# One core, a conv + FFT + FFN hybrid: the nonlinearity's parts in tiles of one writer each, the pooled sum moved to ScalarE, and a new order of issue

## The chip, the cores and the metric

The kernel runs on one core of a Trainium2 chip. The metric is the device time of one execution in microseconds (us), lower is better. Engines are named as in the profile: PE (TensorE matmul), PEld (TensorE weight load), DVE (VectorE), ACT (ScalarE), POOL (GpSimd), SP (SyncE, which here only issues DMAs).

## What is computed

32 images of 56 x 56 pixels with 96 channels go through two layers, all in float32 except for a quantised feed-forward part. The reference, cut to what matters:

```python
# layer 0, per image: mixture weights from the pooled image
pooled = mean(x, axis=(1, 2))
rw = sigmoid(pooled @ Wr + br)                      # 4 experts
h = relu(bn(x @ Wk(rw) + rw @ bpw))                 # 96 -> 384
h = relu(bn(depthwise3x3(h, sum_e rw_e * Wdw_e)))   # 384 channels
x = bn(h @ Wk2(rw) + rw @ bpwl) + x                 # 384 -> 96
# layer 1, tokens t = x as (3136, 96)
u = relu(bn(layernorm(t) @ w1))                     # 96 -> 192
X = fft(u, over the 3136 tokens)
xr = relu(X.real * rd - X.imag * idg + rb)          # rd, idg: diagonals
xi = relu(X.imag * rd + X.real * idg + ib)
t = t + bn(ifft(xr + 1j * xi).real @ w2)            # 192 -> 96
n = layernorm(t)
t = t + qlinear(relu(qlinear(n, W1)), W2)           # 96 -> 384 -> 96, fp8 e5m2 operands
```

## The kernel before

The image is the outer loop of every stage, and several images are in flight at once, each in another stage. The stages of one image, with the names that the profile shows:

- `mixing`: the image `x` is summed over its 3136 pixels (`pooled`), spread over 128 partitions (`pool_b`), multiplied by `wr_s` on PE (`ps_rw`, one small matmul per image, so it marks the beat of the loop), passed through Sigmoid, and turned into the mixed weights `wk`, `small` and `wk2` by DVE.
- `expansion`: `ps_pw` on PE, evacuated by ACT with Relu into `hp` (128 channels x 34 columns x 56 rows, three channel chunks, half an image `p` at a time).
- depthwise: five of the seven blocks of channel chunks 0 and 1 run as 32 x 32 matmuls with diagonal weights on PE (`ps_dw`, three waves of 144 matmuls per image, evacuated by four ACT Relus each into `h2`; the trace calls it `h`). Chunk 2 and two blocks of chunk 1 run on DVE: ACT makes the first tap, DVE adds eight more with `scalar_tensor_tensor` (`h<-hp,small,h`, sizes 1792, 1344 and 896), ACT applies the Relu.
- `projection`: `ps_pwl`, added to the image by DVE.
- `forward` (two streams, each with every other strip of an image): transposes `ps_t_a`, statistics `st_a`, `dm_a`, `rstd_a`, matmul `ps_w` (`w1c`), `ha` on DVE, first DFT `ps_a`, `g` by ACT, out to DRAM (`gd`).
- `frequencies`: `g2` comes back from DRAM (`g<-gd`), the second DFT `ps_b` runs in two groups of frequencies (16 and 13) and three `kind`s of 128 rows each, and the nonlinearity above follows: ACT makes two affine images of the real part and `|idg * im|`, DVE two multiply-adds with the imaginary part, POOL one addition, ACT a Relu, DVE two final operations into `z`. `spectrum` then multiplies by `w2` (`ps_w<-w_s,z`) and makes the first inverse DFT (`ps_c`, via `zo`, to DRAM as `yd`).
- `inverse` (two streams): `yt` from DRAM, `ps_d`, the second layernorm (`ps_t_f`, `st_f`, `nt`, `ps_n`, `n`), the feed-forward (`ps_f` with three hidden chunks `h` that go ACT copy, DVE bias and Relu, POOL cast to fp8, then PE again), the sum, and the store.

PSUM is one pool of four buffers of two banks, shared by all stages: every matmul group takes one, and it comes free when ACT or DVE has evacuated it.

What sets the order: engines execute their queues in order, and the queues are filled by a planner (`class Plan`) at build time. Each stage is a generator that yields the engine it wants next, the events it needs and the buffers it takes. `Plan.run` always takes the stream that could start first by the planner's own costs (`Engine.__getattr__`), with `SLACK` per engine deciding what counts as a tie, and the stream's `priority` number breaking ties. `arrives` gives the planned landing of a DMA. `psum` (line 322 and on) fills each gap that the planner expects on PE: for a planned gap above 0.3 us it issues one filler matmul (112 x 112, result unused) per 0.19 us into the PSUM buffer that was just taken, ahead of the real matmul. The planner's costs are fixed per operation; for a DVE `scalar_tensor_tensor` of n elements they are 0.13 + n / 960 us.

In the nonlinearity before, both parts of a kind share two tiles: `z` (real and imaginary results side by side) and `mir` (two buffers, real and imaginary side by side). ACT writes the real half of `mir`, DVE the imaginary half, and one ACT Relu (n = 896) covers both. The wait is stated in the code:

```python
yield ACT, [("im", n, kind)]
A.activation(m[:, 0:nk, :], m[:, 0:nk, :], AF.Relu)
```

and PE may not start `ps_b` of group n before the last matmul that reads `z` of group n - 1:

```python
yield PE, [("g2 here", n)] + [("z read", n - 1)] * (n >= 1), 1
```

Nearly all instructions are recorded through one helper, so DVE, ACT and POOL work has line L289 and matmuls L585 (transposes L589, fillers L328). Groups are told apart by tile names.

Of the kernel before, what the change touches and what calls it, by code (L numbers as in the profile page):

```python
# [40 lines left out]
F32 = mybir.dt.float32  # L41
# [7 lines left out]
C = 96  # L49
# [84 lines left out]
class Plan:  # L134
# [7 lines left out]

    TAIL = {PE: 0.2, DVE: 0.12, ACT: 0.14, POOL: 0.1, SP: 0.0}


    SLACK = {PE: 0.05, DVE: 0.2, ACT: 0.1, POOL: 1.2, SP: 0.0}

    def __init__(self, **buffers):
        self.free = dict.fromkeys((PE, DVE, ACT, POOL, SP), 0.0)
# [26 lines left out]
        self.buffers[tag].append(self.now if at is None else at)  # L176
        self.buffers[tag].sort()

    def release_after(self, n, used):

        used.append(self.now)
        if len(used) == n:
            self.release(at=max(used))

    def idle(self):

# [62 lines left out]
class Engine:  # L249
# [12 lines left out]
    def __getattr__(self, name):  # L262
        def issue(out, *args, **kw):
            n, port = _size(out), self.port
            if self.engine == DVE:
                us = 0.13 if n > 32 else 0.08
                if name in ("tensor_reduce", "bn_stats"):
                    n = _size(args[0])
                    us = 0.06 if name == "bn_stats" else us
                elif name == "tensor_scalar" and out.dtype == F16:  # L270
                    n, port = n / 4, True
                us += n / 960.0
            elif self.engine == ACT:
                us = 0.05 if name == "copy" else 0.24 if {"scale", "bias"} <= kw.keys() else 0.15
                us += n / 1200.0
                if {"scale", "bias"} <= kw.keys():
                    us = max(us, 0.36)

                asked = [f for f in args[1:] if f in (AF.Sqrt, AF.Sigmoid)]
                if asked and asked != self.loaded:  # L280
                    us += 1.28
                    self.loaded = asked
            elif self.engine == POOL:
                port = name != "memset"
                us = 0.1 + n * {"tensor_copy": 1.04, "memset": 0.6}.get(name, 2.3) / 1000.0
            else:
                us = 0.36
            self.plan.tick(self.engine, us, port)
            return getattr(self.namespace, name)(out, *args, **kw)  # L289

        return issue
@with_exitstack
def kernel(
# [274 lines left out]
    def as_halves(ap):  # L568
        return ap.rearrange("p (j t) -> p j t", j=2)

    plan = Plan(ps=4, mir=2, zo=1, h16=4, x1=NX1)

    V, W, A, P, Q = (
        Engine(plan, DVE, nc.vector), Engine(plan, DVE, nc.vector, True), Engine(plan, ACT, nc.scalar),
# [14 lines left out]
        nc.tensor.transpose(to, ap, eye)  # L589

    def arrives(nbytes, *key):
        plan.done(*key, late=1.4 + nbytes / 220e3)

    mixed, small_of, wk2s, gds, yds, zs, x1s = {}, {}, {}, {}, {}, {}, {}

# [9 lines left out]
    def mixing():  # L605

        for b in range(NB):
            yield DVE, [("x", b)] + [("x1", b - 2, s) for s in range(NS) if b >= 2]
            pooled = mixp.tile([C, 1], F32, tag="pooled", name=f"pooled_{b}")
            V.tensor_reduce(pooled, xs[b], AX.X, ALU.add)  # L610
            pool_b = mixp.tile([C, 128], F32, tag="pool_b", name=f"pool_b_{b}")
            V.behind.tensor_scalar(pool_b, ones, pooled, 1.0 / N, ALU.mult, ALU.mult)
# [23 lines left out]
            small_of[b] = small  # L636
            plan.done("wk", b)
            for c in range(NPE):
                plan.spawn("diagonals", 3, diagonals(b, c))
            yield DVE  # L640
            wk2 = mixp.tile([128, NC3, C], F32, tag="wk2", name=f"wk2_{b}")
            V.tensor_scalar_mul(wk2, wpwl_s[:, 0], rw[:, 0:1])
# [32 lines left out]
    def expansion():  # L675

        for b, p, before in parts_of_all():
            xb = xpad[b % 2]
            for c in (2, 0, 1):

                for part, (at, ns) in enumerate((((0, (9, 9)), (18, (8, 8))), ((0, (8, 8)), (16, (9,))))[p]):
                    yield PE, [("wk", b)] + (readers(*before, c) if before else []), 1
                    wk = mixed[b]
                    ps = psum(f"ps_pw_{b}_{p}_{c}_{part}")
                    for j, n in enumerate(ns):
                        lo = (G * BW * p + at + j * n) * S
                        mm(
                            ps[:, 512 * j : 512 * j + n * S],
                            wk[:, 128 * c : 128 * c + 128],
                            xb[:, lo : lo + n * S],  # L690
                        )
                    plan.spawn("evac pw", 3, expanded(b, p, c, part, at, ns, ps))
            plan.done("exp", b, p)

    def expanded(b, p, c, part, at, ns, ps):
# [14 lines left out]
    def convolved_tensor():  # L710

        for b, p, before in parts_of_all():
            for i, wave in enumerate(WAVES[p]):
# [21 lines left out]

                plan.tick(PE, 0.4)
                plan.done("dwt", b, p, i)
                plan.spawn("evac dw", 6, convolved(b, p, i, wave, ps))

    def convolved(b, p, i, wave, ps):  # L740
        for q, (c, k) in enumerate(wave):
# [38 lines left out]
    def projection():  # L780

        for b, p, _ in parts_of_all():
            needs = [("h2t", b, p, i) for i in range(len(WAVES[p]))] + [("wk2", b)]
            needs += [("h2v", b, p, c) for c, *_ in ON_VECTOR[p]]
            for s, blocks in (((0, (0, 1)), (1, (2, 3))), ((2, (4, 5)), (3, (6,))))[p]:
# [3 lines left out]
                for c in range(NC3):  # L789
                    for j, k in enumerate(blocks):  # L790
# [150 lines left out]
    def frequencies():  # L941


        n = 0
        flat = g2.rearrange("p k m -> p (k m)")
        for b in range(NB):
            for i, (k0, nk) in enumerate(GROUPS):
                for kind in range(NKIND):
                    yield PE, [("g2 here", n)] + [("z read", n - 1)] * (n >= 1), 1
                    ps = psum(f"ps_b_{b}_{k0}_{kind}")  # L950
                    size = (nk + (kind < 2)) // 2
                    for j in range(size):
                        at = 2 * CH * j + 128 * kind
                        mm(ps[:, 128 * j : 128 * j + PB], flat[:, at : at + 128], dftb_s)
                    plan.spawn("nonlinearity", 4, nonlinearity(n, b, k0, size, kind, ps))
                plan.done("g2", n)
                plan.spawn("spectrum", 4, spectrum(n, b, i, k0, nk))
                n += 1

    def nonlinearity(n, b, k0, nk, kind, ps):  # L960
        rd, idg, rb, ib = (nl_s[:, j, kind : kind + 1] for j in range(4))
        nr = nrd[:, kind : kind + 1]
        re = slots(ps, 128, nk, 128, S)
        im = ps[:, 0 : nk * 128].rearrange("p (n w) -> p n w", w=128)[:, :, S:PB]
        yield ACT
        zt = sp.tile([128, GK, PB], F32, tag=f"z_{kind}", name=f"z_{b}_{k0}_{kind}")
        zs[n, kind] = zt
        zr, zi = zt[:, 0:nk, 0:S], zt[:, 0:nk, S:PB]
        A.activation(zi, re, AF.Identity, scale=idg, bias=ib)
        first = k0 == 0 and kind < 2  # L970
        if first:
            A.activation(zr, re, AF.Identity, scale=rd, bias=rb)
# [5 lines left out]
        used = []  # L978
        m = sp.tile([128, GK, PB], F32, tag="mir", name=f"mir_{b}_{k0}_{kind}", bufs=2)
        mr, mi = m[:, 0:nk, 0:S], m[:, 0:nk, S:PB]  # L980
        plan.spawn("imaginary parts", 0, imaginary_parts(n, kind, im, zi, mi, rd, nr, used))
        if not first:
            A.activation(zr, re, AF.Identity, scale=rd, bias=rb)
# [11 lines left out]
        plan.release("mir")  # L995
        plan.done("z", n, kind)

    def imaginary_parts(n, kind, im, zi, mi, rd, nr, used):
        yield DVE
        V.scalar_tensor_tensor(mi, im, nr, zi, ALU.mult, ALU.add)  # L1000
        V.behind.scalar_tensor_tensor(zi, im, rd, zi, ALU.mult, ALU.add)
        plan.release_after(2, used)
        plan.done("im", n, kind)

    def spectrum(n, b, i, k0, nk):

        for at in range(0, nk, GK):
            some = min(GK, nk - at)
            needs = [("z", n, kind) for kind in range(NKIND)] + [("y", n - 1)] * (n >= 1)
# [40 lines left out]
    def inverse(parity):  # L1050


        for b in range(NB):
            for s in range(parity, NS, 2):
# [47 lines left out]
                for c in range(NC3):  # L1102
                    yield PE, (), 1
                    ps = psum(f"ps_f1_{b}_{s}_{c}")
                    for j in range(2):
# [5 lines left out]
                    plan.spawn("hidden", 2, hidden(parity, b, s, c, ps, h8))  # L1111
# [163 lines left out]
```

## Time and profile before

| | us |
|---|---|
| median of three runs | 4427.69 (4416.8 to 4431.31) |
| the profiled execution, own time | 4422.13 |
| its span in the profile | 4420.3 |
| PE busy | 4143.1 |
| DVE busy | 3481.1 |
| ACT busy | 2596.1 |
| POOL busy | 1097.7 |
| PE busy / span, 0 to 215 us | 166.17 / 215.00 |
| PE busy / span, 215 to 4149 us | 3724.15 / 3934.00 |
| PE busy / span, 4149 to 4420 us | 252.83 / 271.00 |

The middle row pair is the loop at full depth; the first and the last rows are the pipeline filling and draining. One image takes about 133 us there (the small matmul `ps_rw` comes at 2194.6, 2326.3 and 2460.9 us). "Busy" merges overlapping instructions of one engine. A matmul in float32 shows as two records in the profile.

### The profile page before, as it was taken

The numbers are of one execution on the slowest core, as the hardware profiler recorded it, in microseconds if no ns is written. First come the engines' busy times: TensorE is split into PE (matmuls) and PEld (weight loads), VectorE is DVE, ScalarE is ACT, GpSimd is POOL, SyncE is SP. The second block draws the span as 40 slices with busy tenths as digits, with TensorE's granted clock in tenths as the row PEclk, the third lists the DMA queues.
The fourth block names the chain that finished last, engine by engine and source line by source line (L and its number), as shares of the span: only waits on it lengthen the run. The fifth ranks groups of instructions, "written<-read, shape, count | busy, mean of one in ns | idle before, by whom it ended". The sixth has DMA issues, their size and how long they took to land.

```text
span 4420.3 us, 119618 instructions
## 1 busy us (share of the span) xinstructions
PE 4143.1 (94%) x50924; PEld 2786.6 (63%) x50924; DVE 3481.1 (79%) x7224; ACT 2596.1 (59%) x4103; POOL 1097.7 (25%) x1015
## 2 busy tenths in 40 slices
PE   6989999999999999999999999999999999999999
PEld 4556666666666666666666666666666666665678
DVE  6778787878787888787787788787888788888763
ACT  2455666656565656566556666556666556666554
POOL 2012232222232221332222332222332222332222
PEclk9999999999999999999999999999999999999999
DMA  3343344433434433444433443433444433434431
GB/s 87 75 105 83 90 100 105 99 104 82 102 97 105 99 103 79 106 99 99 103 92 84 109 103 98 107 88 88 105 107 102 103 92 85 115 96 102 98 98 51
DMA packets 336040, 424.85 MB, mean 96 GB/s; under 512 B 134928, under 2 KB 254544, under 8 KB 332208
## 3 DMA queue, kind: packets, MB, share of 16 engines
q1 hardware_dynamic: 333172, 417.00, 37.6%
q8 instruction: 401, 6.57, 0.6%
q14 instruction: 131, 1.07, 0.1%
q10 hardware_dynamic: 2336, 0.20, 0.0%
HBM read 202.60 MB, written 205.06 MB: 92 GB/s over the span
## 4 chain that ended last, share of the span: by engine, by line
PE 55%; DVE 18%; ACT 12%; DMA 8%; issue 4%; POOL 2%; SPq 0%; ACTq 0%; POOLq 0%; DVEq 0%
PE ps_w L585 11%; PE ps_dw L585 8%; PE ps_pwl L585 8%; DVE h L289 8%; PE ps_pw L585 8%; PE ps_b L585 6%; DMA g<-gd 5%; PE ps_d L585 4%; ACT nt L289 3%; ACT h L289 3%; DVE z L289 3%; DVE ha L289 3%; DMA gd<-g 2%; PE ps_f L585 2%; POOL h L289 2%
## 5 line engine op out<-in xcount | busy, mean ns | idle before, releaser
L289 DVE SCALAR_TENSOR_TENSOR h<-hp,small,h 128x1792 f32<-128x1792 f32 (+2 forms) x768 | 1318.1, 1716 | 56.9 <-ACT h L289 43.6
L585 PE MATMUL ps_dw<-hp,diag 32*32 32x448 f32 x27648 | 884.1, 545 | 31.5 <-issue 26.2
L289 POOL CAST h<-h 128x784 fp8e5<-128x784 f16 x384 | 544.5, 1443 | 1389.1 <-DVE h L289 1387.5
L585 PEld LDWEIGHTS ps_dw<-hp,diag 32*32 32x32 f32 x27648 | 524.8, 103 | 330.9 <-issue 136.8
L585 PE MATMUL ps_pw<-x,wk 96*128 96x448 f32 (+1 forms) x1344 | 594.5, 567 | 12.5 <-ACT y L289 12.0
L289 ACT ACTIVATE hp<-ps_pw,small 128x896 f32<-128x896 f32 (+2 forms) x384 | 360.4, 947 | 385.9 <-PE ps_pw L585 385.5
L585 PE MATMUL ps_pwl<-h,wk 128*96 128x448 f32 x1344 | 528.0, 540 | 0.3 <-ACT hp L289 0.2
L585 PE MATMUL ps_b<-dftb_s,g 112*128 112x112 f32 x2816 | 372.0, 295 | 45.0 <-DMA g<-gd 37.5
L585 PEld LDWEIGHTS ps_w<-w_s,z 128*112 128x112 f32 (+1 forms) x2816 | 352.6, 178 | 88.1 <-ACT h L289 55.2
L585 PEld LDWEIGHTS ps_b<-dftb_s,g 112*128 112x128 f32 x2816 | 356.8, 209 | 81.5 <-ACT h L289 40.5
L585 PE MATMUL ps_w<-w_s,z 128*112 128x96 f32 (+2 forms) x2816 | 372.3, 286 | 33.0 <-ACT h L289 32.4
L585 PEld LDWEIGHTS ps_pwl<-h,wk 128*96 128x96 f32 x1344 | 213.8, 163 | 263.0 <-issue 262.2
L289 ACT ACTIVATE nt<-yt,nm,rstd_f 112x96 fp8e5<-112x96 f32 x896 | 331.3, 456 | 69.6 <-DVE nm L289 69.2
L585 PEld LDWEIGHTS ps_pw<-x,wk 96*128 96x128 f32 x1344 | 238.8, 191 | 200.8 <-issue 140.5
L585 PE MATMUL ps_w<-w1c,x 96*64 96x192 f32 x3584 | 340.3, 332 | 2.4 <-ACT g L289 1.4
L289 ACT ACTIVATE z<-ps_b,nl_s 128x448 f32<-128x448 f32 (+2 forms) x384 | 248.6, 692 | 159.8 <-PE ps_b L585 159.7
L289 ACT CAST h<-ps_f 128x784 f16<-128x784 f32 x384 | 292.7, 820 | 84.3 <-PE ps_f L585 81.8
L289 DVE SCALAR_TENSOR_TENSOR ha<-ps_w,rstd_a,nshift 128x192 f32<-128x192 f32 x896 | 309.7, 407 | 25.8 <-PE ps_w L585 21.5
L289 POOL TENSOR_TENSOR mir<-mir,z 128x448 f32<-128x448 f32 (+1 forms) x192 | 203.7, 1061 | 482.0 <-ACT mir L289 364.3
L289 POOL TENSOR_TENSOR x<-x,y 96x784 f32<-96x784 f32 x128 | 258.1, 2021 | 261.5 <-DVE y L289 261.5
L289 ACT ACTIVATE h<-ps_dw,small 128x448 f32<-128x448 f32 x384 | 223.5, 628 | 134.6 <-PE ps_dw L585 134.6
L289 DVE SCALAR_TENSOR_TENSOR x<-ps_pwl,small,x 96x896 f32<-96x896 f32 (+1 forms) x128 | 131.5, 1027 | 209.2 <-PE ps_pwl L585 209.2
(167 smaller groups left out, 5727.3 us busy)
## 6 DMA issues: line engine op xcount, KB each, us to landing
gd<-g SPq DMA_DIRECT2D x448, 192.0 KB
g<-gd SPq DMA_DIRECT2D x64, 672.0 KB
x<-in_x_dram SPq DMA_DIRECT2D x32, 1176.0 KB
x<-x SPq DMA_DIRECT2D x128, 294.0 KB
yt<-yd SPq DMA_DIRECT2D x128, 294.0 KB
out_dram<-x SPq DMA_DIRECT2D x128, 294.0 KB
g<-gd SPq DMA_DIRECT2D x64, 546.0 KB
x<-x SPq DMA_DIRECT2D x96, 336.0 KB
```

What stands on the lines that cost most here:

```text
L289: return getattr(self.namespace, name)(out, *args, **kw)
L585: nc.tensor.matmul(to, lhsT, rhs, start=start, stop=stop)
```

## The change

Four things change, and the order of issue follows from all of them, since the planner decides it:

1. The nonlinearity writes four tiles per kind, `nl0` to `nl3`, contiguous, two buffers each, with one writer engine at a time per part. The real and the imaginary part are two independent chains, each with its own Relu on ACT (12 Relus of half the size per image in place of 6) and its own final operation into `z`. The correction `dc` of the zero frequency becomes two additions of one column instead of one addition of two. `z` is taken only when its final operation is issued, and only that operation waits for the reader of the group before; PE's `ps_b` keeps this wait for the last of the three kinds alone.
2. `pooled` comes from an ACT copy of `x` onto itself with an accumulator output, in place of a DVE reduction.
3. The planner multiplies every cost but PE's matmuls (which tick directly) by `MARGIN = 1.07`; SLACK of DVE goes from 0.2 to 0.3 and of ACT from 0.1 to 0.05; a DMA is planned at 2.0 us + bytes / 190e3 per us instead of 1.4 us + bytes / 220e3.
4. Most priorities get other numbers.

The diff, cut to its core:

```diff
+    MARGIN = 1.07
+
-    SLACK = {PE: 0.05, DVE: 0.2, ACT: 0.1, POOL: 1.2, SP: 0.0}
+    SLACK = {PE: 0.05, DVE: 0.3, ACT: 0.05, POOL: 1.2, SP: 0.0}
...
-            self.plan.tick(self.engine, us, port)
+            self.plan.tick(self.engine, us * self.plan.MARGIN, port)
...
-    plan = Plan(ps=4, mir=2, zo=1, h16=4, x1=NX1)
+    plan = Plan(ps=4, nl=2, zo=1, h16=4, x1=NX1)
...
-        plan.done(*key, late=1.4 + nbytes / 220e3)
+        plan.done(*key, late=2.0 + nbytes / 190e3)
...
-            yield DVE, [("x", b)] + [("x1", b - 2, s) for s in range(NS) if b >= 2]
+            yield ACT, [("x", b)] + [("x1", b - 2, s) for s in range(NS) if b >= 2]
...
-            V.tensor_reduce(pooled, xs[b], AX.X, ALU.add)
+            A.activation(xs[b], xs[b], AF.Copy, accum_out=pooled)
+            yield DVE
...
-                plan.spawn("diagonals", 3, diagonals(b, c))
+                plan.spawn("diagonals", 7, diagonals(b, c))
...
-                    plan.spawn("evac pw", 3, expanded(b, p, c, part, at, ns, ps))
+                    plan.spawn("evac pw", 6, expanded(b, p, c, part, at, ns, ps))
...
-                plan.spawn("evac dw", 6, convolved(b, p, i, wave, ps))
+                plan.spawn("evac dw", 1, convolved(b, p, i, wave, ps))
...
-                plan.spawn("evac prj", 6, projected(b, s, blocks, ps))
+                plan.spawn("evac prj", 2, projected(b, s, blocks, ps))
...
-                    yield PE, [("g2 here", n)] + [("z read", n - 1)] * (n >= 1), 1
+                    yield PE, [("g2 here", n)] + [("z read", n - 1)] * (n >= 1 and kind == 2), 1
...
+        u, w, mr, mi = (
+            sp.tile([128, GK, S], F32, tag=f"nl{j}", name=f"nl{j}_{b}_{k0}_{kind}", bufs=2)[:, 0:nk]
+            for j in range(4)
+        )
+        used, over = [], []
+        A.activation(w, re, AF.Identity, scale=idg, bias=ib)
+        imaginary = imaginary_parts(n, b, k0, nk, kind, im, w, mi, used, over)
+        if k0 == 0 and kind < 2:
+            A.activation(u, re, AF.Identity, scale=rd, bias=rb)
             yield DVE
             n0 = CH - 128 if kind else 128
-            at0 = zt[:n0, 0, 0 : S + 1 : S]
-            V.tensor_add(at0, at0, dc[:n0, kind, :])
-        yield ACT, (), "mir"
+            V.tensor_add(u[:n0, 0, 0:1], u[:n0, 0, 0:1], dc[:n0, kind, 0:1])
+            V.tensor_add(w[:n0, 0, 0:1], w[:n0, 0, 0:1], dc[:n0, kind, 1:2])
...
         A.activation(mr, im, AF.Abs, scale=idg)
         plan.release_after(2, used)
         yield POOL
-        P.tensor_add(mr, mr, zr)
-        yield ACT, [("im", n, kind)]
-        A.activation(m[:, 0:nk, :], m[:, 0:nk, :], AF.Relu)
-        yield DVE
-        W.scalar_tensor_tensor(zr, zr, 2.0, mr, ALU.mult, ALU.max)
-        W.scalar_tensor_tensor(zi, zi, 0.0, mi, ALU.max, ALU.subtract)
+        P.tensor_add(mr, mr, u)
+        yield ACT
+        A.activation(mr, mr, AF.Relu)
+        yield DVE, [("z read", n - 1)] * (n >= 1)
+        zr = spectrum_of(n, b, k0, kind)[:, 0:nk, 0:S]
+        W.scalar_tensor_tensor(zr, u, 2.0, mr, ALU.mult, ALU.max)
+        plan.release_after(2, over, "nl")
+        plan.done("z", n, kind, 0)
+
+    def imaginary_parts(n, b, k0, nk, kind, im, w, mi, used, over):
         yield DVE
+        V.scalar_tensor_tensor(mi, im, nrd[:, kind : kind + 1], w, ALU.mult, ALU.add)
+        V.behind.scalar_tensor_tensor(w, im, nl_s[:, 0, kind : kind + 1], w, ALU.mult, ALU.add)
         plan.release_after(2, used)
+        yield ACT
+        A.activation(mi, mi, AF.Relu)
+        yield DVE, [("z read", n - 1)] * (n >= 1)
+        zi = spectrum_of(n, b, k0, kind)[:, 0:nk, S:PB]
+        W.scalar_tensor_tensor(zi, w, 0.0, mi, ALU.max, ALU.subtract)
...
-            ("loads", 8, loads()), ("mixing", 6, mixing()), ("inverse", 1, inverse(0)),
-            ("inverse", 0, inverse(1)), ("frequency loads", 0, frequency_loads()),
-            ("frequencies", 1, frequencies()), ("forward", 0, forward(0)),
-            ("forward", 0, forward(1)), ("projection", 7, projection()),
-            ("vector", 5, convolved_vector()), ("tensor", 2, convolved_tensor()),
-            ("expansion", 7, expansion()),
+            ("loads", 2, loads()), ("mixing", 5, mixing()), ("inverse", 6, inverse(0)),
+            ("inverse", 0, inverse(1)), ("frequency loads", 4, frequency_loads()),
+            ("frequencies", 6, frequencies()), ("forward", 0, forward(0)),
+            ("forward", 1, forward(1)), ("projection", 8, projection()),
+            ("vector", 6, convolved_vector()), ("tensor", 2, convolved_tensor()),
+            ("expansion", 9, expansion()),
```

`spectrum_of` makes the `z` tile of a kind at its first use, and `release_after` gets the buffer's tag as an argument. In the built programs the matmuls of the stages are the same in number; the order is not (nearly every row differs), and the fillers go from 467 to 794.

More of the change, by code (lines that the diff above doesn't have):

```diff
@@ L177, in release, with release_after @@
         self.buffers[tag].sort()
-    def release_after(self, n, used):
+    def release_after(self, n, used, tag="ps"):
         used.append(self.now)
         if len(used) == n:
-            self.release(at=max(used))
+            self.release(tag, max(used))
     def idle(self):
@@ L607, in mixing @@
         for b in range(NB):
-            yield DVE, [("x", b)] + [("x1", b - 2, s) for s in range(NS) if b >= 2]
+            yield ACT, [("x", b)] + [("x1", b - 2, s) for s in range(NS) if b >= 2]
             pooled = mixp.tile([C, 1], F32, tag="pooled", name=f"pooled_{b}")
-            V.tensor_reduce(pooled, xs[b], AX.X, ALU.add)
-            pool_b = mixp.tile([C, 128], F32, tag="pool_b", name=f"pool_b_{b}")
-            V.behind.tensor_scalar(pool_b, ones, pooled, 1.0 / N, ALU.mult, ALU.mult)
+            A.activation(xs[b], xs[b], AF.Copy, accum_out=pooled)
+            yield DVE
+            pool_b = mixp.tile([C, 128], F32, tag="pool_b", name=f"pool_b_{b}", bufs=1)
+            V.tensor_scalar(pool_b, ones, pooled, 1.0 / N, ALU.mult, ALU.mult)
             rw = mixp.tile([128, NE + 1], F32, tag="rw", name=f"rw_{b}")
@@ L954, in frequencies @@
                         mm(ps[:, 128 * j : 128 * j + PB], flat[:, at : at + 128], dftb_s)
-                    plan.spawn("nonlinearity", 4, nonlinearity(n, b, k0, size, kind, ps))
+                    plan.spawn("nonlinearity", 3, nonlinearity(n, b, k0, size, kind, ps))
                 plan.done("g2", n)
-                plan.spawn("spectrum", 4, spectrum(n, b, i, k0, nk))
+                plan.spawn("spectrum", 3, spectrum(n, b, i, k0, nk))
                 n += 1
@@ L961, in nonlinearity @@
         rd, idg, rb, ib = (nl_s[:, j, kind : kind + 1] for j in range(4))
-        nr = nrd[:, kind : kind + 1]
         re = slots(ps, 128, nk, 128, S)
         im = ps[:, 0 : nk * 128].rearrange("p (n w) -> p n w", w=128)[:, :, S:PB]
[L965 to L972, printed above, removed]
+        yield ACT, (), "nl"
+        u, w, mr, mi = (
[7 more added lines that the diff above has]
+            A.activation(u, re, AF.Identity, scale=rd, bias=rb)
             yield DVE
             n0 = CH - 128 if kind else 128
-            at0 = zt[:n0, 0, 0 : S + 1 : S]
-            V.tensor_add(at0, at0, dc[:n0, kind, :])
-        yield ACT, (), "mir"
[L978 to L983, printed above, removed]
+            V.tensor_add(u[:n0, 0, 0:1], u[:n0, 0, 0:1], dc[:n0, kind, 0:1])
+            V.tensor_add(w[:n0, 0, 0:1], w[:n0, 0, 0:1], dc[:n0, kind, 1:2])
+            yield ACT
+            plan.spawn("imaginary parts", 5, imaginary)
+        else:
+            plan.spawn("imaginary parts", 2, imaginary)
+            A.activation(u, re, AF.Identity, scale=rd, bias=rb)
         A.activation(mr, im, AF.Abs, scale=idg)
@@ L988, in nonlinearity, with spectrum_of @@
         yield POOL
-        P.tensor_add(mr, mr, zr)
-        yield ACT, [("im", n, kind)]
-        A.activation(m[:, 0:nk, :], m[:, 0:nk, :], AF.Relu)
-        yield DVE
-        W.scalar_tensor_tensor(zr, zr, 2.0, mr, ALU.mult, ALU.max)
-        W.scalar_tensor_tensor(zi, zi, 0.0, mi, ALU.max, ALU.subtract)
-        plan.release("mir")
-        plan.done("z", n, kind)
-    def imaginary_parts(n, kind, im, zi, mi, rd, nr, used):
-        yield DVE
-        V.scalar_tensor_tensor(mi, im, nr, zi, ALU.mult, ALU.add)
-        V.behind.scalar_tensor_tensor(zi, im, rd, zi, ALU.mult, ALU.add)
-        plan.release_after(2, used)
-        plan.done("im", n, kind)
+        P.tensor_add(mr, mr, u)
[7 more added lines that the diff above has]
+    def imaginary_parts(n, b, k0, nk, kind, im, w, mi, used, over):
+        yield DVE
+        V.scalar_tensor_tensor(mi, im, nrd[:, kind : kind + 1], w, ALU.mult, ALU.add)
+        V.behind.scalar_tensor_tensor(w, im, nl_s[:, 0, kind : kind + 1], w, ALU.mult, ALU.add)
+        plan.release_after(2, used)
+        yield ACT
+        A.activation(mi, mi, AF.Relu)
+        yield DVE, [("z read", n - 1)] * (n >= 1)
+        zi = spectrum_of(n, b, k0, kind)[:, 0:nk, S:PB]
+        W.scalar_tensor_tensor(zi, w, 0.0, mi, ALU.max, ALU.subtract)
+        plan.release_after(2, over, "nl")
+        plan.done("z", n, kind, 1)
+    def spectrum_of(n, b, k0, kind):
+        if (n, kind) not in zs:
+            zs[n, kind] = sp.tile([128, GK, PB], F32, tag=f"z_{kind}", name=f"z_{b}_{k0}_{kind}")
+        return zs[n, kind]
     def spectrum(n, b, i, k0, nk):
@@ L1008, in spectrum @@
             some = min(GK, nk - at)
-            needs = [("z", n, kind) for kind in range(NKIND)] + [("y", n - 1)] * (n >= 1)
+            needs = [("z", n, kind, j) for kind in range(NKIND) for j in range(2)] + [("y", n - 1)] * (n >= 1)
             yield PE, needs + [("yt read", b - 2, s) for s in range(NS) if b >= 2], 1
@@ L1110, in inverse @@
                         )
-                    plan.spawn("hidden", 2, hidden(parity, b, s, c, ps, h8))
+                    plan.spawn("hidden", 1, hidden(parity, b, s, c, ps, h8))
                 yield PE, [("h8", b, s, c) for c in range(NC3)], 1
```

## The prediction

> **What bounds the kernel now.** I read the page's first part, then two stretches of one image each, then PE's waits over the loop at full depth, then the groups by shape that the change touches.
>
> ```profile
> PE 4143.1 (94%) x50924; PEld 2786.6 (63%) x50924; DVE 3481.1 (79%) x7224; ACT 2596.1 (59%) x4103; POOL 1097.7 (25%) x1015
> ...
> PEclk9999999999999999999999999999999999999999
> ```
>
> ```profile
> 2193.40:2267.50 74.10, 70.77 (x724) 48.43 (x723) 64.88 (x136) 48.98 (x77) 20.79 (x21) 1.00 0.31 75
> 2267.50:2326.40 58.90, 55.77 (x855) 35.41 (x853) 44.03 (x90) 33.20 (x55) 13.57 (x11) 1.00 0.49 120
> ```
>
> The columns of the second fence are the stretch and its length, then busy us of PE, PEld, DVE, ACT, POOL, then the clock and DMA. The two rows are one image: the first ends when DVE's last tap of the vector convolution is done, the second at the next `ps_rw`. PE works 126.5 of 133.0 us and sets the beat; DVE is near it in the first part (64.88 of 74.10) and has room in the second (44.03 of 58.90). The clock is full, so filler matmuls have nothing more to win. So the change can only win what PE idles, about 7 us per image. The waits say for whom (us in total, times, longest), from 215 to 4149 us:
>
> ```profile
> PE ps_b L585 <- DMA g<-gd: 33.3, 21, 3.1
> PE ps_w L585 <- ACT h L289: 32.4, 28, 1.5
> PE ps_f L585 <- POOL h L289: 32.0, 28, 1.2
> PE ps_dw L585 <- issue: 24.7, 26, 2.2
> PE ps_t_f L589 <- ACT hp L289: 23.0, 28, 0.9
> PE ps_f L585 <- ACT h L289: 14.7, 60, 1.4
> PE ps_f L585 <- DVE ha L289: 12.4, 28, 0.4
> PE ps_pw L585 <- ACT y L289: 10.9, 16, 1.1
> ...
> PE ps_b L585 <- ACT h L289: 7.1, 5, 2.6
> PE ps_f L585 <- ACT zo L289: 5.6, 28, 0.2
> ```
>
> They add up, with 7.7 us for one late `yt`, to 204 of the 210 us that PE idles in this stretch (3934.00 less 3724.15). No wait is large: each is a transfer or an evacuation that came about 1 us later than the planner thought, once per image (28 times in 29.5 beats). Why the planner is early:
>
> ```profile
> L289 DVE SCALAR_TENSOR_TENSOR h<-hp,small,h 128x1792 f32<-128x1792 f32 x256 | 579.0, 2262 | 7.9 <-ACT h L289 4.3
> ...
> L289 DVE TENSOR_REDUCE pooled<-x 96x1 f32<-96x3136 f32 x32 | 108.9, 3405 | 8.0 <-DMA x<-in_x_dram 8.0
> ...
> L289 ACT ACTIVATE mir<-mir 128x896 f32<-128x896 f32 x96 | 91.1, 949 | 18.8 <-POOL mir L289 17.8 <-DVE mir L289 0.4
> ...
> L289 ACT ACTIVATE h<-h,small 128x1792 f32<-128x1792 f32 x32 | 57.2, 1789 | 230.2 <-DVE h L289 230.2
> ...
> L328 PE MATMUL ps_f<-dftb_s 112*112 112x112 f32 x244 | 26.3, 263 | 0.2 <-ACT h L289 0.2
> ```
>
> The planner gives the 1792-element tap 0.13 + 1792/960 = 2.00 us, the chip took 2.262 (13% more).
>
> **What the Trainium skill says.** "SBUF — State Buffer", section "SBUF: two separate sides": a DVE operation with two SBUF inputs and a GpSimd operation that reads SBUF exclude each other on one shared port for a whole instruction. The trace agrees: taps of 1344 elements took 1.61 us alone and up to 2.1 each (two in 4.29 us) while POOL worked; the planner models the exclusion but starts from too short a cost. "TensorE: Matmul & The Clock Gate", section "What's actually happening", says that PE's clock falls after an idle window of about 3.4 us; the loop's longest wait but one is 3.1 us and the clock is 0.97 to 1.00, so fillers buy nothing. "Perfetto Trace Analysis", section "Optimization Strategy", says that an equal gap that repeats can mean too few buffers; here it is four PSUM buffers whose evacuations queue on ACT.
>
> **The change, part by part.**
>
> Pooled sum. DVE loses 32 x 3.405 = 109 us. ACT gains an operation that the trace doesn't have: "ScalarE: Activation LUTs", section "What ACT_TABLE_LOAD costs", prices immediate operands at 186 ns + 0.833 ns per element, an estimate of 2.80 us for 3136; its price with a pointer operand (280 + 0.833 x 1792 = 1773 ns) meets the trace's 1789. Bounds 2.8 to 3.1 us (plus one small ACT operation like `rstd_f`, 0.29, if the accumulator is read apart); I take 2.8, so 90 us on ACT. In the built order it stands behind the first evacuation of the half image, beside the 4.7 us of `ps_pwl`, with `y` and three `hp` evacuations queued behind it; `ps_rw` and the next `ps_pw` wait for those. Cover gone, it costs PE up to 3 us per image.
>
> Split Relus. 192 of 752 to 949 ns become 384 of half the size: 0.56 us by that page's price, 0.63 by the trace's 448-element rows. Per pair 0.17 to 0.31 us more, I take 0.2: 38 us on ACT. The `dc` additions go from 64 to 128 of 0.155 us: +10 us on DVE. So DVE is 3481 - 109 + 10 = 3382 (76%), ACT 2596 + 90 + 38 = 2724 (62%). PE stays the bound, and neither sum moves the span by itself.
>
> One writer per tile. DVE waited 112.4 us for ACT's `mir` (152 times, waits of all engines): its multiply-add needs only the first ACT operation but stood behind ACT's third. In the new order it waits only for the first. That is 3.5 us of DVE bubbles per image, nearly all in the first part, where DVE is close to PE. It moves the end only through what follows on DVE.
>
> Fillers. In the built order the old loop has none at full depth; the new one has 10 per image, the same for 29 images: 3 ahead of `ps_pw_0_2_0`, 1 ahead of the last spectrum matmul, 6 ahead of `ps_pw_0_1_0`. A filler takes 26.3 / 122 = 0.216 us (244 records are 122 matmuls). 290 x 0.216 = 63 us if PE had other work, nothing if it would have waited; I take 63. The other 37 new ones lie in the fill and the drain, where PE waits for longer: 0.
>
> New order, waits that go. `g<-gd`: a landing takes 9 to 11 us by the chain of waits; the first `ps_b` of an image stood behind one wave (8.7 us) and some 4 us more after the last strip, and now about 30 us later: -33.3. `ps_w<-ACT h`: after a wave the ACT queue held one Relu, then a Relu that waits for DVE's taps, a first tap, and only then the second Relu that frees the PSUM buffer; now the two Relus are adjacent and the waiting one is moved: -32.4. `ps_f<-POOL h`: 7.1 us of PE work between the third hidden matmul and its reader, now 6.7, 12.0, 9.1 and 4.9 in the four places; copy 0.82, bias 0.41 to 0.62, cast 1.44 fit: -32.0. `ps_t_f<-ACT hp`, `ps_pw<-ACT y`, `ps_b<-ACT h`, `ps_f<-ACT zo`: all are buffers freed by an ACT queue that the margin plans later: -23.0 - 10.9 - 7.1 - 5.6. Sum -144.3. Issue (24.7), the three hidden matmuls in a row (14.7 + 12.4) and `yt` stay.
>
> New waits. I walked the new DVE order with the trace's durations from the addition of `ps_d_3` to the last 896-element tap: taps 8 x 1.74 + 8 x 1.15, four `ha` groups 5.5, statistics 5.5, nonlinearity 13.5, biases 5.2, `zo` 2.6, the rest 3.4: 58.8 us. PE has 58.0 us there, and 2.1 of fillers. They are level, so DVE comes in late at a few places: `ps_t_f_2` (0.7), `ps_a_0_0` (0.4), `ps_a_2_4` in the second part (0.6). 1.7 x 29.5 = +50 us.
>
> Sum, against the profiled execution: 4422 - 144 + 63 + 50 = 4391. The median lies 5.6 us above that execution (0.1%), so I say 4395.
>
> **Rivals.**
>
> Slower: DVE becomes the bound of the first part. In the old order it idled 9.2 of these 74.1 us behind in-order waits; if 4 us of such bubbles stay in the new 58.8, DVE needs 62.8 where PE has 60.1, and PE stands at `ps_pw_0_1_0`, behind its six fillers, for the 2.7 us on top: 29.5 x 3 = +89, so 4480. It decides from 1.3 us of bubbles on. For it: the taps still cost 5% more than the planner's cost times 1.07. Against: the freed `mir` wait.
>
> Faster: the fillers fall into waits that would be there anyway and half of the new waits don't come: 4391 - 25 - 31 = 4335, say 4340. For it: two of the three places are where PE waits for the vector taps.
>
> No change: with four PSUM buffers and the same work the 1 us waits form again elsewhere: 4422 - 144 + 144, within 0.3%.
>
> That the new order doesn't do what it says has little room: it is what the build gives.
>
> **How the numbers follow.** Forecast 0.35 (own range 4365 to 4412), faster rival 0.20, no change 0.12, slower rival 0.33. A measurement tells about 0.3% here, 13 us around 4428. So faster 0.55, same 0.12, slower 0.33. The range takes in most of both rivals and ends at 4325 and 4490.
>
> **What would show it.** Right: `ps_b<-DMA`, `ps_w<-ACT h` and `ps_f<-POOL h` gone from PE's waits; TENSOR_REDUCE gone, an ACT row of 2.8 us; DVE's waits for ACT in the nonlinearity well below 112; PE busy near 4206. Wrong: PE waiting for DVE's `h` ahead of `ps_pw`, or for ACT behind the pooled copy, by over 2 us per image.

## The result and the profile after

| | before | after |
|---|---|---|
| median of 20 runs each, us | 4426.01 (4409.01 to 4438.1) | 4443.2 (4424.09 to 4454.81) |
| the profiled execution, own time | 4422.13 | 4424.09 |
| its span | 4420.3 | 4422.3 |

The ratio is 1.0039, 95% interval 1.0029 to 1.005: the change made the kernel 0.4% slower. The forecast was 4395 and faster. The profiled execution of after is the fastest of its 20, 19 us under their median, so its trace shows a mild case of what follows.

The page of after, busy times of the engines and the share of the instruction queue:

```profile
PE 4160.7 (94%) x51578; PEld 2841.8 (64%) x51578; DVE 3385.6 (77%) x7256; ACT 2697.5 (61%) x4360; POOL 968.2 (22%) x1015
...
q8 instruction: 406, 6.65, 0.7%
```

DVE landed within 4 us of the sum made for it (3382), ACT 27 us under its own (2724). PE was busy 17.6 us longer, far less than the forecast's 63. The second line is a DMA queue that brings instructions: packets, MB and the time that they took. PE's records (51578 matmuls and as many weight loads) come to 254 for each of its 406 packets of 16.4 KB, so I take it to be PE's own. It becomes important below.

The loop at full depth, one row of the view by stretches (length, then busy us of PE, PEld, DVE, ACT, POOL, the clock and DMA):

```profile
215.00:4149.00 3934.00, 3733.58 (x46450) 2521.61 (x46452) 3076.41 (x6553) 2465.75 (x3980) 870.63 (x906) 0.99 0.38 97
```

PE idles 200 us in this stretch where it idled 210. PE's longest waits in the same stretch (us in total, times, longest):

```profile
PE ps_dw L587 <- issue: 69.4, 38, 3.9
PE ps_a L587 <- DVE ha L291: 24.2, 29, 0.8
PE ps_d L587 <- DMA yt<-yd: 23.0, 23, 1.9
PE ps_pw L587 <- ACT yt L291: 19.2, 29, 0.7
PE ps_t_f L591 <- DVE x L291: 18.1, 29, 0.7
PE ps_a L587 <- ACT h L291: 12.4, 29, 0.4
PE ps_n L587 <- DVE nl L291: 12.2, 29, 0.4
PE ps_pw L330 <- ACT h L291: 6.8, 29, 0.2
PE ps_w L587 <- ACT h L291: 6.8, 29, 0.2
PE ps_d L587 <- ACT h L291: 3.0, 4, 1.0
PE ps_b L587 <- DMA g<-gd: 0.7, 1, 0.7
```

Read against the list of before, the change did what it set out to do: the waits of `ps_b` for `g`, of `ps_f` for POOL's `h`, and those behind `hp`, `y` and `zo` are gone or nearly so. Two things took their place. One is a set of small waits, most of them exactly once per image (29 times, at most 0.2 to 0.8 us each). The other heads the list: PE stands in the middle of a depthwise wave with no engine and no transfer that it waits for ("issue"), 69.4 us in 38 gaps of up to 3.9 us; before it was 24.7 in 26.

**One such gap.** The timeline of after around one wave (start, length, engine, line, operation, count, in brackets the idle time before it):

```profile
2338.93 0.88 SPq L291 DMA_DIRECT2D g<-gd  x2
2339.28 6.96 PE L587 MATMUL ps_dw<-hp,diag 32*32 32x448 f32 x233
...
2349.08 2.82 PE L587 MATMUL ps_dw<-hp,diag 32*32 32x448 f32 x55 [2.85 <-issue]
```

The view by stretches over the same time:

```profile
2339.00:2343.00 4.00, 4.00 (x138) 2.59 (x138) 2.54 (x8) 1.86 (x3) 0.86 (x2) 1.00 0.68 136
2343.00:2346.20 3.20, 3.20 (x117) 1.92 (x99) 3.16 (x4) 1.09 (x2) 1.13 (x1) 1.00 0.97 172
2346.20:2349.10 2.90, 0.05 (x7) 0.02 (x4) 2.87 (x5) 0.00 (x0) 1.76 (x1) 1.00 0.09 15
```

In the new order SP issues the load of the second frequency group (`g<-gd`, two DMAs of 546 KB, together 1.12 MB) 0.35 us before the wave of the second half image starts. The 16 DMA engines then fill to 97% (the number before the last), and by the time they fall idle PE has stopped, after 233 of the wave's 288 records. It is so in every image: 29 waves of the trace have this load issued 0.35 us ahead of them, and they hold 64.6 of the 69.4 us of gaps; all other waves together hold 4.8. The DMA view of two of these stretches, 2339 to 2346.2 us and then the gap (packets, MB, share):

```profile
q1 hardware_dynamic: 1439, 1.09, 80.9%
...
q1 hardware_dynamic: 45, 0.03, 5.8%
q8 instruction: 1, 0.02, 3.0%
```

While the DMA engines were full only data moved; the one packet of instructions is sent and lands in the gap, when the load is all but over. In the trace of before the same wave of an image runs from 2243.92 to 2252.72 us without a break. The same view there, for 2243.5 to 2248 and for 2248 to 2252.6 us:

```profile
q1 hardware_dynamic: 259, 0.65, 53.1%
q8 instruction: 1, 0.02, 1.3%
...
q8 instruction: 1, 0.02, 1.2%
```

There a packet of instructions comes in each half of the wave. A wave is a dense piece of PE's program: 576 instructions (288 matmuls and weight loads each) in 8.8 us. "Runtime: NRT & Kernel Launch" of the Trainium skill, section "Instruction fetch mechanics", says that an engine fetches its instructions in blocks of 16 KiB, 256 instructions, through a DMA queue of its own while it executes the block before. The packet size in the trace agrees. The section calls the cost "mostly hidden"; in this wave it is not.

The packets say what PE waited for. In the gap above, the instruction packet has landed at 2347.63 us and PE goes on at 2349.08, 1.45 us later. All 38 gaps of after end in this way, 1.2 to 1.7 us after an instruction packet has landed, and so do the 27 of before in its whole span; a moment picked at random would lie that close behind a packet in about 5% of cases. So the gaps of before, which the prediction left as they were, are of the same kind: 17 of these 27 come within 12 us of the issue of the next image's load (1176 KB).

So the theory to be tested (theory 1): **the new order puts a 1.12 MB load on a depthwise wave, and PE's instructions come late behind it.** Rivals: the 280 fillers cost the time (theory 2), or the pooled copy on ACT delays what stands behind it (theory 3).

### The profile page after: what moved, and what is told of

It reads as the page before. It is cut to its first block, busy times and chain, and to the rows that moved or that the text cites. A ratio compares the mean times of both kernels' runs of the same rounds, so it can differ in the third digit from the quotient of the medians.

```text
span 4422.3 us, 121145 instructions
## 1 busy us (share of the span) xinstructions
PE 4160.7 (94%) x51578; PEld 2841.8 (64%) x51578; DVE 3385.6 (77%) x7256; ACT 2697.5 (61%) x4360; POOL 968.2 (22%) x1015
## 4 chain that ended last, share of the span: by engine, by line
PE 78%; DVE 7%; DMA 6%; ACT 5%; issue 3%; SPq 1%; ACTq 0%; POOL 0%; POOLq 0%; DVEq 0%
PE ps_dw L587 20%; PE ps_w L587 11%; PE ps_pw L587 10%; PE ps_pwl L587 9%; PE ps_b L587 6%; PE ps_f L587 5%; PE ps_c L587 3%; DMA yt<-yd 3%; PE ps_d L587 3%; PE ps_a L587 3%; ACT h L291 3%; PE ps_t_f L591 2%; DMA yd<-zo 2%; DVE ha L291 2%; PE ps_pw L330 1%
## 5 line engine op out<-in xcount | busy, mean ns | idle before, releaser
L587 PE MATMUL ps_dw<-hp,diag 32*32 32x448 f32 x27648 | 886.0, 552 | 70.0 <-issue 69.4
L291 POOL CAST h<-h 128x784 fp8e5<-128x784 f16 x384 | 367.3, 970 | 1431.5 <-DVE h L291 1431.5
L587 PE MATMUL ps_pw<-x,wk 96*128 96x448 f32 (+1 forms) x1344 | 585.4, 568 | 19.8 <-ACT yt L291 19.8
L291 ACT ACTIVATE nl<-ps_b,nl_s 128x448 f32<-128x448 f32 (+2 forms) x576 | 347.4, 661 | 150.2 <-PE ps_b L587 86.9
L291 POOL TENSOR_TENSOR x<-x,y 96x784 f32<-96x784 f32 x128 | 291.4, 2277 | 582.1 <-DVE y L291 578.5
L291 POOL TENSOR_TENSOR nl<-nl,nl 128x448 f32<-128x448 f32 (+1 forms) x192 | 221.9, 1156 | 757.1 <-ACT nl L291 743.0
L587 PE MATMUL ps_b<-dftb_s,g 112*128 112x112 f32 x2816 | 351.8, 277 | 7.4 <-DMA g<-gd 4.6
L587 PEld LDWEIGHTS ps_b<-dftb_s,g 112*128 112x128 f32 x2816 | 335.5, 193 | 27.8 <-ACT h L291 10.4
L291 DVE TENSOR_SCALAR h<-h,fb 128x784 f16<-128x784 f16 x384 | 229.9, 613 | 140.4 <-ACT h L291 137.9
```

Source lines behind the costliest of these rows:

```text
L587: nc.tensor.matmul(to, lhsT, rhs, start=start, stop=stop)
```

## The experiments

Each was timed in five rounds together with the kernel before on the same chip; ratios are to that kernel.

**The second group's load left out.** The load of the second frequency group is not made for any image but the first; SP's time stays in the plan, so that every other queue is the same. The second group is then computed from the first group's data.

```diff
 for c in range(2):
+    if i == 1 and b:
+        plan.tick(SP, 0.36 * plan.MARGIN)
+        continue
     Q.dma_start(
```

> The changed kernel, with the load of the second frequency group into g2 left out for every image but the first (its planned time on SP is kept, so all other queues hold the same instructions in the same order; the second group is then computed from the first group's data). Theory 1 (PE's instruction fetch waits behind that load, which now starts together with a depthwise wave): PE's wait ps_dw <- issue falls from 69 to below 30 us, and the time falls by 35 to 50 us, so about 4400 where the changed kernel has 4443 (ratio to the kernel before 0.993 to 0.997). Theory 2 (the fillers cost their full 63 us and the load is innocent): the wait ps_dw <- issue stays near 69, and the time stays within 10 us of 4443 (ratio 1.002 to 1.006). Theory 3 (the pooled sum on ACT holds up PE): as theory 2.

Measured: 4332.71 us, ratio 0.9791 (0.9775 to 0.9806). PE's waits of this run over the loop (215 to 4060 us):

```profile
PE ps_d L587 <- DMA yt<-yd: 24.3, 25, 2.0
PE ps_a L587 <- DVE ha L291: 24.1, 29, 0.8
PE ps_pw L587 <- ACT yt L291: 19.8, 30, 0.7
PE ps_t_f L591 <- DVE x L291: 18.8, 29, 0.7
...
PE ps_dw L587 <- issue: 4.5, 8, 0.8
```

The gaps are nearly gone and no other wait in the list has moved by more than 1.3 us. The depthwise groups, after and this run (busy, mean ns, idle before):

```profile
L587 PE MATMUL ps_dw<-hp,diag 32*32 32x448 f32 x27648 | 886.0, 552 | 70.0 <-issue 69.4
```

```profile
L587 PE MATMUL ps_dw<-hp,diag 32*32 32x448 f32 x27648 | 856.8, 543 | 5.2 <-issue 4.5
```

The time fell by 110 us where theory 1 expected 35 to 50, and the difference can be found: 69.4 - 4.5 = 65 us of gaps, and PE was busy 4160.7 - 4130.8 = 30 us less, 29 of them in the waves. Together 95; the spans differ by 4422.3 - 4328.8 = 93.5. (The rest, up to the 110 between the medians, is mostly that after's profile lies 19 us under its median.) Most of the 30 us comes with the clock, which falls right after the gap shown above. The view by stretches of after:

```profile
2349.10:2350.00 0.90, 0.90 (x34) 0.53 (x35) 0.90 (x1) 0.00 (x0) 0.90 (x1) 1.00 0.00 0
2350.00:2353.00 3.00, 3.00 (x43) 1.13 (x25) 1.74 (x1) 1.16 (x2) 0.33 (x1) 0.50 0.59 146
2353.00:2354.00 1.00, 1.00 (x12) 0.52 (x14) 0.00 (x0) 0.17 (x1) 0.00 (x0) 0.79 0.90 322
```

The clock stands at 0.50 for 3 us, and PE does the end of the wave and what follows at half speed. Over the whole run the mean clock is 0.994 in after's profile and 0.998 here. Of after's waves 36.9 us ran at 0.50 and none here, which is 18 of the 29 us; the other 11 stay unexplained.

**The reverse: a load put on that wave in the kernel before.** Two copies of `hp` to a scratch area in DRAM, 1.01 MB each, are issued when the second half's wave starts; nobody reads them.

```diff
 yield PE, needs, 2
+if p == 1:
+    for c in range(2):
+        spare = dram.tile([128, (G * BW + 2) * (S + 2)], F32, tag=f"sp{c}", name=f"spare_{b}_{c}")
+        nc.sync.dma_start(spare, hp[c].rearrange("p w h -> p (w h)"))
 ps = [psum(f"ps_dw_{b}_{p}_{i}_{u}") for u in range(2)]
```

> The kernel before with one added transfer per image: as the depthwise wave of the second half image starts, two tiles of hp (1.01 MB each) are copied to a DRAM buffer that nothing reads. All compute queues are the same. Theory 1 (a transfer that starts with a wave starves PE's instruction fetch): ps_dw <- issue rises from 26 us to 60 us or more, and the time rises by 20 to 60 us, ratio 1.005 to 1.014. Theories 2 and 3 (transfers don't touch PE's instruction supply): ps_dw <- issue stays at 20 to 35 us and the time within 13 us, ratio 0.997 to 1.003.

Measured: 4500.17 us, ratio 1.0175 (1.0156 to 1.0193). PE's waits (whole span) of this run:

```profile
PE ps_dw L585 <- issue: 87.6, 54, 3.3
```

and of before in the same view the waits on issue were 26.2 us. The time rose by 75 us, more than the 20 to 60 expected: besides 61 us of gaps, the mean clock of the profile fell from 0.988 to 0.979, which is some 40 us, while `ps_w<-ACT h` went from 32.4 us to 1.0. One wave of this run in the view by stretches:

```profile
2268.70:2272.50 3.80, 3.80 (x136) 2.44 (x136) 2.85 (x5) 1.89 (x5) 2.59 (x2) 1.00 1.01 365
2272.50:2276.10 3.60, 3.60 (x121) 2.30 (x104) 3.20 (x5) 1.84 (x3) 0.90 (x1) 1.00 0.88 332
2276.10:2278.30 2.20, 0.05 (x1) 0.00 (x0) 2.20 (x4) 0.00 (x0) 0.00 (x0) 1.00 0.01 3
```

It is the picture of after again, made with a transfer whose result nobody reads: full DMA engines for 7.4 us, then an empty PE for 2.2 us. Here too each of the 54 gaps ends 1.2 to 1.7 us after an instruction packet has landed.

**The control: the same kind of copies behind the wave.** Two copies of `h2[0]`, 0.92 MB each, issued once the wave's results have been evacuated.

```diff
 plan.spawn("evac dw", 6, convolved(b, p, i, wave, ps))
+if p == 1:
+    yield SP, [("h2t", b, 1, 0)]
+    for c in range(2):
+        spare = dram.tile([128, G * TB], F32, tag=f"sp{c}", name=f"spare_{b}_{c}")
+        nc.sync.dma_start(spare, h2[0])
```

> The control to before_dummy: the kernel before with about the same bytes copied to DRAM once per image (two copies of one h2 tile, 0.92 MB each), but only after the depthwise wave of the second half image has been evacuated, so the copies run beside other matmuls. Theory 1 (a transfer harms when it overlaps a wave, whose 576 instructions in 8.7 us need the most instruction fetches): ps_dw <- issue stays at 20 to 40 us instead of 82, and the time rises by 0 to 25 us (ratio 1.000 to 1.006), from waits for other transfers. Theory 4 (any added megabytes slow the kernel, wherever they are put, through DRAM or DMA traffic): the time rises by 50 us or more as in before_dummy (ratio above 1.012).

Measured: 4427.96 us, ratio 1.0013 (1.0003 to 1.0023). PE's waits (whole span):

```profile
PE ps_dw L585 <- issue: 26.2, 28, 2.3
```

After the wave that starts at 2246.61 us, for example, the copies are issued at 2261.27 us and run beside matmuls of other stages:

```profile
2261.00:2266.00 5.00, 5.00 (x27) 3.43 (x26) 4.23 (x5) 2.58 (x4) 0.00 (x0) 1.00 0.80 327
```

PE needs 27 matmuls in these 5.0 us, where the wave needed 136 in 3.8, and it doesn't stop. Nearly the same bytes (1.84 MB for 2.02) cost 0.13% here and 1.75% when they lie on the wave. So it is not the traffic as such, it is where it falls. That PE waits for its instructions is shown by the packets; why they are late is not. That the fetch stands behind data *inside* the DMA engines is inferred from the order of the packets; the trace doesn't show when PE's sequencer asks for a block.

**Fillers left out at full depth.** The planner's filler count is forced to 0 from the fourth to the last image (280 fewer); all other queues are the same.

```diff
-for _ in range(min(40, int((plan.idle() - 0.3) / 0.19))):
+beat[0] += name.startswith("ps_rw")
+idle = plan.idle()
+for _ in range(0 if 3 < beat[0] < NB else min(40, int((idle - 0.3) / 0.19))):
```

> The changed kernel without the 10 fillers per image at full depth (280 fillers fewer; fill and drain keep theirs; all other instructions and their order are the same). Theory 2 (the fillers cost PE their full time): 4443 - 60 = 4383, ratio 0.990. Theory 1 (the loss is the instruction fetch; the fillers stand where PE waits for DVE's taps anyway): the time falls by less than 25 us, ratio 0.998 to 1.003, and the waits PE ps_pw <- DVE h or <- ACT h take most of the fillers' place; ps_dw <- issue stays at 60 to 75 us.

Measured: 4395.25 us, ratio 0.9927 (0.9909 to 0.9945), which is 48 us below after's median, 0.17 us per filler. The gaps stay (74.8 us on issue in the whole span, 35 times). Theory 2 is right about a cost and wrong as the explanation: the prediction had counted the fillers, at 63. Theory 1 as written was wrong about the fillers: it expected less than 25 us and other waits in their place. PE's waits other than issue come to 129 us at full depth here (215 to 4149 us) and to 127 in after, so the fillers did not stand in time that PE would have waited.

**The pooled sum back on DVE.** The DVE reduction in place of the ACT copy, with ACT's time kept in the plan and the rest of the order the same.

```diff
-A.activation(xs[b], xs[b], AF.Copy, accum_out=pooled)
+plan.tick(ACT, (0.15 + N / 1200.0) * plan.MARGIN)
+nc.vector.tensor_reduce(pooled, xs[b], AX.X, ALU.add)
```

> The changed kernel with the pooled sum back on DVE as TENSOR_REDUCE (planned as before on ACT, so PE, POOL and SP keep their order; DVE gets 3.4 us per image ahead of pool_b, ACT loses its copy of about 3 us). Theory 3 (the pooled copy on ACT holds up evacuations and so PE): the time falls by 20 us or more, ratio below 1.000. Theory 1 and theory 2: the time stays within 13 us of 4443 or rises a little, ratio 1.001 to 1.008, and ps_dw <- issue stays at 60 to 75 us.

Measured: 4445.87 us, ratio 1.0043 (1.0027 to 1.0059), like after. The gaps stay too (72.3 us on issue). Theory 3 falls: 109 us of DVE work moved to ACT are worth nothing in either direction at this place, within the 0.2% that the intervals allow. PE's order is that of after, and wave by wave so are the gaps: the first four are 2.78, 1.11, 2.62 and 3.89 us here and 3.17, 1.26, 2.73 and 3.71 there. So a gap's length belongs to its place in PE's program; that it depends on where an instruction block ends in the wave would fit, and was not tested.

**The old planner with the new tiles.** Parts 1 and 2 of the change stay; `MARGIN` 1.0, the old SLACK, the old DMA landing and all old priorities (those of the new generators 0).

```diff
-    MARGIN = 1.07
-    SLACK = {PE: 0.05, DVE: 0.3, ACT: 0.05, POOL: 1.2, SP: 0.0}
+    MARGIN = 1.0
+    SLACK = {PE: 0.05, DVE: 0.2, ACT: 0.1, POOL: 1.2, SP: 0.0}
...
-        plan.done(*key, late=2.0 + nbytes / 190e3)
+        plan.done(*key, late=1.4 + nbytes / 220e3)
```

> Parts 1 and 2 of the change alone: the tiles of one writer and the pooled sum on ACT, with the planner's constants and all priorities as before (no margin). In the order that this gives, the last ps_b of the first frequency group stands some 50 us of PE work ahead of the next wave, so the second group's load overlaps none. Theory 1: ps_dw <- issue stays below 35 us. Theory 5 (the loss lies in the tiles and the pooled sum themselves): the time is 20 us or more above the kernel before with issue waits low, and the waits on PE name nl or x on ACT. If the new order's gain in other waits is due to the margin, this kernel has the late evacuations of the kernel before back (ps_f <- POOL h, ps_w <- ACT h, 20 us or more each) and is within 30 us of 4425 or slower.

Measured: 4837.76 us, ratio 1.0945 (1.093 to 1.096), with `yt` (88.5 us), `dm_a` (45.4) and `issue` (39.7) at the head of PE's waits. Theory 1 missed here: it expected issue below 35. At full depth none of the gaps comes within 12 us of a load of `g` being issued, but 24 of all 28 do so of the image's load; all of them end 1.2 to 1.7 us after an instruction packet has landed. The two late evacuations that were to come back without the margin did not (`ps_f<-POOL h` is gone, `ps_w<-ACT h` is at 3 us), so their going is not shown to be the margin's doing. About parts 1 and 2 by themselves this run says little, since the old priorities were chosen for other streams. What each part is worth alone stays open.

**Other orders, chosen to keep loads off the waves.** Two builds of after with other priorities, no fillers at full depth, and chosen among many plans for little planned overlap of the loads with the waves: order_a (margin 1.07, overlap at most 0.6 us per image where after has 7) and order_d (margin 1.10, SLACK of DVE 0.1, of ACT 0, of POOL 0.8). The core of order_a:

```diff
-            ("loads", 2, loads()), ("mixing", 5, mixing()), ("inverse", 6, inverse(0)),
-            ("inverse", 0, inverse(1)), ("frequency loads", 4, frequency_loads()),
+            ("loads", 4, loads()), ("mixing", 7, mixing()), ("inverse", 6, inverse(0)),
+            ("inverse", 6, inverse(1)), ("frequency loads", 1, frequency_loads()),
...
-            ("vector", 6, convolved_vector()), ("tensor", 2, convolved_tensor()),
-            ("expansion", 9, expansion()),
+            ("vector", 8, convolved_vector()), ("tensor", 3, convolved_tensor()),
+            ("expansion", 8, expansion()),
```

> The changed kernel with another set of priorities and SLACK values (margin still 1.07), chosen so that in the planner's own times neither frequency load nor the image load overlaps a depthwise wave by more than 0.6 us per image (7 us in the changed kernel), and without fillers at full depth. Theory 1: ps_dw <- issue falls below 25 us and the time to 4330 to 4390 (the changed kernel without fillers had 4395 with 75 us of issue waits). If the issue waits fall and the time doesn't, other waits took their place, and PE's list will name them.

> As order_a, with priorities chosen under a margin of 1.10 instead of 1.07 (planned overlap of loads with waves 0.5 us per image), again without fillers at full depth. Theory 1: ps_dw <- issue below 25 us, time 4320 to 4390. If planning with slower engines makes the waits for ACT, DVE and POOL rarer, these sum to less than the 130 us that the changed kernel has at full depth, and order_d is below order_a; if the margin says nothing of the chip, order_d has as many as order_a or more.

Measured: order_a 4326.78 us, ratio 0.9777 (0.9761 to 0.9793), faster than both kernels and 68 us below after without its fillers, with all loads and the whole computation in place. No wave has a load of `g` issued at its start any more. Its waits in the loop (215 to 4050 us):

```profile
PE ps_rw L591 <- ACT y L291: 23.4, 29, 1.1
PE ps_t_a L591 <- DVE dm_a L291: 22.3, 29, 0.8
PE ps_c L591 <- ACT zo L291: 17.3, 51, 1.3
...
PE ps_dw L591 <- issue: 3.1, 7, 0.9
```

order_d: 4547.61 us, ratio 1.0275 (1.0258 to 1.0292), far above the 4320 to 4390 expected. Its gaps are gone too, but one wait alone eats more than they cost (215 to 4149 us):

```profile
PE ps_d L591 <- DMA yt<-yd: 140.8, 28, 5.9
```

Keeping loads off the waves doesn't make an order good: order_a gained with it, order_d lost more elsewhere. The planner gives `yt` the same landing formula as in after, and here the data come up to 5.9 us later than PE needs them. The larger margin didn't help either: PE's waits for ACT, DVE and POOL at full depth come to 163 us, against 85 in order_a and 103 in after (the 130 of the expectation took in the waits for DMAs).

## Why the prediction was wrong, step by step

| term, 215 to 4149 us | predicted | measured |
|---|---|---|
| waits said to go | -144 | -137 |
| `ps_f` behind `h` and `ha`, said to stay (14.7 + 12.4) | 0 | -27 |
| new waits that were named (`ps_t_f`, `ps_a` behind DVE) | +50 | +42 |
| new waits not named (`yt`, `ps_pw`, `ps_a` behind ACT, `ps_n`, small ones) | 0 | +69 |
| issue | 0 | +45 |
| sum of PE's idle time | -94 | -8 |
| fillers | +63 | +48 |
| time that PE loses at half clock | 0 | -26 |

PE's busy time gives -9 for the idle time (210 to 200). The last row is from after's profile, which is a mild one. The rows come to +14 us where the spans of the two profiles differ by +2: fill and drain idle 6 us less, and the rest is not settled.

- **The step that failed is "Issue (24.7), the three hidden matmuls in a row and `yt` stay".** Issue nearly tripled, to 69.4 us: the 45 us more, with the slower clock behind the gaps, are what turned the sign. As an estimate, 65 us of gaps went with 95 us of time in the run without the load, so 45 us stand for some 66, and 4443 less 66 is 4377, faster than before and near the forecast. The prediction did look at the load of `g`, and only as something that PE waits *for*. It moved the first `ps_b` of an image some 30 us back from its load, which is why `ps_b<-DMA g<-gd` went, as predicted. It didn't ask what PE does while a load is running.
- That the other terms come so near the forecast is in part luck: 69 us of waits that were not named and 7 that did not go stand against 27 of `ps_f`, 26 of the clock, 15 of the fillers and 8 of the new waits that were named.
- "The clock is full" was a misreading, and a term put at nothing. The old loop had 17 stretches at half clock that cost PE 48 us of work, and 15 of them came behind a wait of 1.5 us or more, most often that for `g`. One of them, with PE waiting from 1649.94 to 1651.64 us, in the view by stretches of before:

```profile
1649.95:1651.60 1.65, 0.00 (x0) 0.00 (x0) 0.00 (x0) 1.65 (x3) 1.65 (x2) 1.00 0.08 18
1652.80:1656.10 3.30, 3.30 (x18) 3.30 (x17) 0.16 (x1) 1.71 (x3) 0.28 (x1) 0.50 0.98 294
```

  In after's profile 12 such stretches cost 22 us, 11 of them behind gaps in waves. So the waits that went were worth more than their length, and so were the gaps that came.
- The waits that go: right in mechanism and size. Only `ps_w<-ACT h` left a rest, 6.8 of 32.4.
- The new waits: those that the walk along DVE's queue named came near (`ps_t_f` 18.1 for a predicted 0.7 x 29 = 20; `ps_a` behind DVE 24.2, at one place of 0.8 us, for 29 at two places). The walk was made for DVE only. Most of what it missed sits on other queues: `ps_pw` behind ACT, 0.7 us in each image, `ps_a` behind ACT, 0.4, and `yt`, which came late 23 times instead of rarely; `ps_n` behind DVE's `nl`, 0.4, lay on DVE and was missed too. These 69 us are a term that was left short; the mechanism of late evacuations was known.
- The fillers: 0.17 us each instead of 0.216. The 0.216 was read from merged busy time; the waits did not grow where the fillers went, so it is the price that was too high, and the faster rival's "waits that would be there anyway" is not what happened.
- PE busy was forecast at 4206 and is 4160.7. The fillers are there (48 us), so the other matmuls were busy some 30 us less. The clock accounts for 26 of it; the rest is not settled. In the medians this gain is smaller: after's 20 runs mostly show a clock of 0.988 to 0.991.
- The pooled sum: the copy takes 2.85 us, where the price from "ScalarE: Activation LUTs" of the Trainium skill gave an estimate of 2.80, and it moves the end by nothing:

```profile
L291 ACT ACTIVATE x<-x 96x3136 f32<-96x3136 f32 x32 | 91.1, 2847 | 0.0
```

- One writer per tile: "well below 112" was wrong for the row it was read from and right for the group. DVE's multiply-add into the third tile (`mir` before, `nl` after) waits 102 us for ACT where it waited 112. What went is the wait of the two `dc` additions, 172.5 us before and 27.7 after, which the prediction had not looked at. Neither is on PE's path.
- The slower rival gave the right sign for a wrong reason: PE doesn't stand for DVE ahead of `ps_pw`; the fillers there wait 6.8 us in all, for ACT. Its sum also rounds 2.7 us per image up to 3; with 2.7 it gives 4471 in place of 4480.
- The rival "no change" comes nearest in time (0.39% where it said within 0.3%). New small waits did form, 111 us where 164 went, but its sum leaves out the fillers, and issue was not in it either.

## What to carry to other kernels

When a change moves a transfer, ask two questions of it: who waits for it, and what runs beside it. In this kernel a long burst of small instructions needed its instruction stream, and a load of a megabyte on top of it stopped the engine although nothing in the program made it wait. It showed as idle time on "issue", and as a packet of the instruction queue that landed only when the data were through, 1.2 to 1.7 us before the engine went on. In a planned order such a collision is a cost that the planner doesn't know: either give it that cost, or pick among equal plans the one whose loads fall beside long instructions.

## What was not expected of the hardware

- A load of 1.12 MB issued with a wave stopped PE for up to 3.9 us, and two copies of 1.01 MB did the same in another kernel (+61 us on issue); 1.84 MB behind the wave did not (0.13% in all).
- In every run here each gap on issue ahead of a `ps_dw` matmul (263 in all) ended 1.2 to 1.7 us after an instruction packet had landed.
- The clock fell to 0.50 for some 3 us after an idle time of 2.85 us in after, and after one of 1.70 us in before. The prediction quoted about 3.4 us as the window; here shorter gaps were enough, and the fall came 0.9 and 1.1 us after PE had resumed. It doesn't follow every such gap: of the 20 gaps of 1.5 us and more in after's waves 11 were followed by it. A gap therefore costs more than its length: with 65 us of gaps, 95 us went.
